# First adder convolution of an image network: TensorE's other work moved to the borders of groups, a group's near slots put side by side, its banks emptied behind the first slot

## The chip, the cores and the metric

The kernel runs on one core of one Trainium2 chip. Its time is the device time of one execution in microseconds, as the median of several runs; lower is better. Beside it there is one profiled execution, from which all durations of instructions are read.

## The reference

Four layers follow each other on an input of 4 images with 128 channels of 64x64. The diff touches the second one (an adder network block), and of that its first half:

```python
def shift_conv(x, w, stride=1):
    wq = shift_quant(w)                       # weights rounded to powers of two
    return lax.conv_general_dilated(x, wq, window_strides=(stride, stride), ...)   # 3x3, pad 1

def adder_conv(x, w):                         # out = -sum |patch - weight|, 3x3, pad 1
    patches = lax.conv_general_dilated_patches(x, filter_shape=(K, K), ...)
    p = patches.reshape(N, Ck, H * W)
    wf = w.reshape(Cout, Ck)
    def per_channel(wc):
        return -jnp.sum(jnp.abs(p - wc[None, :, None]), axis=1)
    out = lax.map(per_channel, wf)
    return out.transpose(1, 0, 2).reshape(N, Cout, H, W)

out = adder_conv(shift_conv(x, w_shift1, stride=1), w_add1)
out = jax.nn.relu(batchnorm(out, bn1_gamma, bn1_beta))
out = adder_conv(shift_conv(out, w_shift2, stride=1), w_add2)
```

So for each location and output channel the absolute differences between 128 x 9 values and weights are summed.

## The kernel before

**Splitting the sum.** A value that lies outside the range of its channel's weights contributes a term that is linear in the weights; only a "live" value, inside the range, needs relu(weight + value) worked out for all 1152 weights (9 taps x 128 output channels) of its channel. Few values are live. `sparse_adder` (L648 to L786) works on that: 32 blocks of 512 locations (8 per image), each of four groups of 128 locations, 128 groups in all. The result of a group is a table of 128 locations x 1152 (tap, output channel), in three PSUM banks of 384 columns.

**What a group does on TensorE.**

- `add_linear` (L601): nine matmuls in bf16, three parts of the weights times three banks, which open the banks.
- `add_near` (L586): for each of four near slots, the l-th live value of every channel in each of four windows of 32 locations. Four "distances" (relu(weight + value), 128x1152) are made by `distance` (L570), two on VectorE (L580) and two on ScalarE (L578), and 12 matmuls add them. These use a quarter of the array's columns each (the form 128*32 in the profile), all others use 128*128. A float32 matmul leaves two records in the profile, so a slot has 24 records.
- `add_far` (L595): three matmuls for live values beyond the four slots, with weights gathered by an indirect DMA from POOL (`weights_of`, L522) and one more distance, on VectorE for even groups and on ScalarE for odd ones.
- `closed` (L609): ScalarE empties the three banks into `ts`, with the group's totals as bias.
- `combine` (L625): nine or twelve matmuls (18 or 24 records) shift `ts` by its taps and add it to an output bank; 4 groups of an image later VectorE finishes the output block (`finished`, L725).

The pool of banks for the tables has five buffers and a group opens three, so the third bank of a group is the first of the group before it. Distances lie in two rings of six buffers, one for each engine: an engine can be three slots ahead of TensorE.

**What finds the live values.** While the four groups of a block run, `found` (L705) prepares the next block, in steps that are taken from a generator between two distances. On TensorE there are the shift convolution (`convolved`, L688, 27 matmuls in bf16), the totals (`totals`, L552), the places in the list (`listed`, L466 to L468) and the list itself (32 small matmuls, L501). On VectorE there are the copy of the convolution (L701), the ranks (L421 to L430), the list's masks and counts (L454 to L464), the totals' operand (L556), the maxima (L471, L472), the near slots (L541 to L545), then, once TensorE has given the places, chairs, fields, value, lanes and the far pattern. `thirds` (L284) splits the input of the block after that into three bf16 parts, by two casts on ScalarE (L289) and two subtractions on VectorE (L290), in turn.

**What sets the order.** Everything in this stage is recorded in program order for its engine, and each engine works through its queue in that order. `beside` (L756) is called after each of the 17 distances of a group and takes steps of `found` at a rate of 88 steps per 68 distances:

```python
                due += of * 88.0 / per
                while due >= 1.0:
                    due -= 1.0
                    next(steps, None)
```

A step that waits for TensorE stands `AFTER = 8` empty steps behind the matmuls that it waits for. TensorE's pieces of `found` go where their step falls, ahead of the near slot whose distances are being made. The closing and the combining of the group before stand behind the second near slot. `found`, the totals, the places and the list share one PSUM bank (`ps_c`).

Of the kernel before, what the change touches and what calls it, by code (L numbers as in the profile page):

```python
# [20 lines left out]
P = 128  # L21
# [262 lines left out]
def thirds(tc, pool, x, name, bufs=2):  # L284

    nc, then = tc.nc, tc.keep_in_program_order
    parts = [pool.tile(x.shape, BF16, tag=f"third{i}", bufs=bufs, name=f"{name}_{i}") for i in range(3)]
    for i in range(2):
        then(nc.scalar.copy(parts[i], x))  # L289
        then(nc.vector.tensor_tensor(x if i == 0 else parts[2], x, parts[i], ALU.subtract))  # L290
    return parts
# [16 lines left out]
TC = TAPS * P // 3  # L308


class Sparse:
# [104 lines left out]
    def ranks(self, q, v):  # L416

        nc, then, u = self.tc.nc, self.tc.keep_in_program_order, f"{self.tag}{q}"
        shape = [P, BK]
        below = self.kp.tile(shape, BF16, tag="below", name=f"below{u}")  # L420
        then(nc.vector.tensor_scalar(below, v, self.low, 2.0, ALU.is_ge, ALU.mult))  # L421
        yield
        t = self.tp.tile(shape, F32, tag="t0", name=f"live{u}")
        then(nc.vector.scalar_tensor_tensor(t, v, self.high, below, ALU.is_gt, ALU.is_gt))
        yield
        rank = self.tp.tile(shape, F32, tag="t1", name=f"rank{u}")
        then(nc.vector.tensor_tensor_scan(rank, self.inside[32], t, 0.0, ALU.mult, ALU.add))
        yield
        near = self.tp.tile(shape, F32, tag="t2", name=f"near{u}")
        then(nc.vector.tensor_tensor(near, rank, t, ALU.mult))  # L430
        yield
        yield below, near
# [12 lines left out]
    def listed(self, q, v, near, counts):  # L445
# [20 lines left out]
        pb = self.ps_c.tile([P, 2, GROUPS], F32, tag="cv", name=f"pbase{u}")  # L466
        then(nc.tensor.matmul(pb[:, 0, :], self.before, full, start=True, stop=False, skip_group_check=True))
        then(nc.tensor.matmul(pb[:, 1, :], self.cm.ones, full, start=False, stop=True, skip_group_check=True))  # L468
        at, where = new(data, "at8"), new(data, "where", U32)
        for j in range(GROUPS):  # L470
            then(nc.vector.max(at[:, j, :], masked[:, bass.ts(j, P)]))  # L471
            then(nc.vector.max_index(where[:, j, :], at[:, j, :], masked[:, bass.ts(j, P)]))  # L472
            yield
            yield
        crowded = self.crowded[:, GROUPS * q : GROUPS * (q + 1)]
        then(nc.vector.tensor_scalar(crowded, pb[:, 1, :], float(P), None, ALU.is_gt))
        base = new(small, "base")
        then(nc.vector.scalar_tensor_tensor(base, crowded, 1000.0, pb[:, 0, :], ALU.mult, ALU.add))
        then(nc.vector.tensor_tensor(counts[:, GROUPS * q : GROUPS * (q + 1)], crowded, count, ALU.mult))
        yield  # L480
        wide = [P, GROUPS, TOP + P]
        chairs = self.lp.tile(wide, BF16, tag="chairs", bufs=2, name=f"chairs{u}")
        then(nc.vector.tensor_tensor(
            chairs, self.chair.unsqueeze(1).broadcast_to(wide), base.unsqueeze(2).broadcast_to(wide), ALU.is_equal
        ))
        yield
# [11 lines left out]
        then(nc.vector.tensor_scalar(what[..., 4], valid, self.lane, None, ALU.mult))  # L498
        yield
        pl = self.ps_c.tile([P, GROUPS, FIELDS], F32, tag="cv", name=f"plist{u}")  # L500
        for j in range(GROUPS):  # L501
            for l in range(TOP):
                then(nc.tensor.matmul(
                    pl[:, j, :], chairs[:, j, TOP - l : TOP - l + P], what[:, j, l, :], start=(j + l == 0),
                    stop=(j == GROUPS - 1 and l == TOP - 1), skip_group_check=True,
                ))
            yield
        for _ in range(AFTER):
            yield
# [9 lines left out]
        yield  # L519
        yield value, lanes, hot  # L520
# [9 lines left out]
    def slots(self, q, v, key, ranks, size, tag, bufs):  # L530

        nc, then, u = self.tc.nc, self.tc.keep_in_program_order, f"{self.tag}{q}"
        n, nw = len(ranks), BK // size
        hot = self.kp.tile([P, n, BK], F32, tag=f"hot{tag}", bufs=bufs, name=f"hot{tag}{u}")
        at = self.kp.tile([P, n, nw], F32, tag=f"at{tag}", bufs=bufs, name=f"at{tag}{u}")
        step = 2
        for l0 in range(0, n, step):
            m = min(step, n - l0)
            hp = self.kp.tile([P, step, BK], F32, tag="hp", bufs=1, name=f"hp{tag}{u}_{l0}")
            for l in range(l0, l0 + m):  # L540
                then(nc.vector.tensor_scalar(hot[:, l, :], key, ranks[l], 2.0, ALU.is_equal, ALU.mult))  # L541
                yield
                then(nc.vector.scalar_tensor_tensor(hp[:, l - l0, :], key, ranks[l], v, ALU.is_equal, ALU.mult))
                yield
            then(nc.vector.tensor_reduce(  # L545
                at[:, l0 : l0 + m, :].rearrange("p l w -> p (l w)"),
                hp[:, :m, :].rearrange("p l (w j) -> p (l w) j", j=size), AX.X, ALU.add,
            ))
            yield
        yield hot, at  # L550

    def totals(self, q, v, below):  # L552

        nc, then, u = self.tc.nc, self.tc.keep_in_program_order, f"{self.tag}{q}"
        sp = self.tp.tile([P, BK], F32, tag="t0", name=f"sp{u}")
        then(nc.vector.scalar_tensor_tensor(sp, below, 1.0, v, ALU.subtract, ALU.mult))  # L556
        yield
        pt = self.ps_c.tile([P, GROUPS], F32, tag="cv", name=f"ptot{u}")
        for j in range(GROUPS):
            then(nc.tensor.matmul(  # L560
                pt[:, j : j + 1], sp[:, bass.ts(j, P)], self.cm.one_col, start=(j == 0), stop=(j == GROUPS - 1),
                skip_group_check=True,
            ))
        for _ in range(AFTER):
            yield
        total = self.kp.tile([P, GROUPS], F32, tag="total", name=f"total{u}")
        then(nc.vector.tensor_copy(total, pt))
        yield total
# [32 lines left out]
    def add_linear(self, t, lhs):  # L601

        for i, part in enumerate(self.w3):
            for y in range(3):
# [42 lines left out]

def sparse_adder(tc, cm, sp, x_d, wqs, stats, counts, p_d, y_d, tag):  # L648
# [9 lines left out]
    with ExitStack() as ctx:  # L658
# [23 lines left out]
        def split(q):  # L682
            if q < blocks:
                parts[q] = thirds(tc, xin_pool, xins.pop(q), f"{tag}x3{q}")

        split(0)

        def convolved(q):  # L688
            xins[q + 2] = fetch(q + 2)
            here = parts.pop(q)  # L690
            b, k = divmod(q, NB)
            pc = sp.ps_c.tile([P, BK], F32, tag="cv", name=f"{tag}pc{q}")
            for t in range(TAPS):
                shifted(tc, pc, wqs, here, t)
                yield
            split(q + 1)
            yield
            for _ in range(AFTER):
                yield
# [3 lines left out]
            yield v  # L703

        def found(q):  # L705

            def last_of(g):
                v = None
                for v in g:
                    if v is None:  # L710
                        yield
                got.append(v)

            got = []
            yield from last_of(convolved(q))
            v, = got
            yield from last_of(sp.ranks(q, v))
            below, near = got[1]
            yield from last_of(sp.totals(q, v, below))
            yield from last_of(sp.slots(q, v, near, near_ranks, 32, "n", 2))  # L720
            yield from last_of(sp.listed(q, v, near, counts))
            value, lanes, hot = got[4]
            ready[q] = (below, got[2], *got[3], value, lanes, hot)
# [14 lines left out]
        per = (S_NEAR * 4 + 1) * GROUPS  # L738

        ripe = []  # L740

        def combined(m, t, total):
            b, n = divmod(m, N // P)
            sp.combine(b, n, sp.closed(t, m, total))
            ripe.extend([AFTER, b, k] for k in sp.done(n))

        steps, due = iter(()), 0.0
        for m in range(groups):
            q, j = divmod(m, GROUPS)
            if j == 0:  # L750
                for _ in steps:
                    pass
                below, total, hot_n, at_n, value, lanes, hot_l = ready.pop(q)
                steps = found(q + 1) if q + 1 < blocks else iter(())

            def beside(of):  # L756
                nonlocal due
# [5 lines left out]
                due += of * 88.0 / per  # L763
                while due >= 1.0:
                    due -= 1.0
                    next(steps, None)

            t = sp.open_rows(m)
            weights = sp.weights_of(lanes[:, j : j + 1], m)
            sp.add_linear(t, below[:, bass.ts(j, P)])  # L770
            for l in range(S_NEAR):
                rs = []
                for g in range(4):
                    w = 4 * j + g
                    rs.append(sp.distance(g % 2 == 1, at_n[:, l, w : w + 1], f"n{m}_{l}_{g}"))
                    beside(1)
                sp.add_near(t, lambda g: hot_n[:, l, P * j + 32 * g : P * j + 32 * g + 32], lambda g: rs[g], False)
                if l == 1 and waiting is not None:
                    combined(*waiting)
            r = sp.distance(m % 2 == 1, value[:, j : j + 1], f"l{m}", weights)  # L780
            beside(1)
            sp.add_far(t, hot_l[:, j, :], r, False, True)
            waiting = (m, t, total[:, j : j + 1])
        combined(*waiting)
# [4 lines left out]
def sparse_rest(tc, cm, sp, left, stats, p_d, y_d, tag):  # L789
# [5 lines left out]
    with ExitStack() as ctx:  # L795
# [4 lines left out]
        with tc.For_i(0, left, F):  # L800
            with ExitStack() as inner_ctx:
# [3 lines left out]
                for q in range(B * NB):  # L805
# [3 lines left out]
                    *_, (_, near) = sp.ranks(f"r{q}", v)  # L809
# [4 lines left out]
                    *_, (hot, at) = sp.slots(f"r{q}", v, far, ranks, P, "f", 1)  # L814
# [100 lines left out]
class Sorted(Sparse):  # L915
# [75 lines left out]
    def arranged(self, s, wqs, load):  # L991
# [4 lines left out]
        def fetch(k):  # L996
# [9 lines left out]
            def third():  # L1006
                landed()
                return thirds(self.tc, self.xp, t, f"x3{u}_{k}", 1)
# [1784 lines left out]
```

## Time and profile before

| | us |
|---|---|
| median of 3 runs | 13672.89 (13670.84 to 13677.84) |
| the profiled execution | 13709.18 |
| its span, first to last instruction | 13707.2 |
| mean granted TensorE clock of that execution | 0.951 |
| near slots of the first adder convolution, first to last | 2055.3 to 4228.3 |
| in 3500 to 4000: TensorE busy | 482.39 |
| in 3500 to 4000: VectorE busy | 342.64 |
| in 3500 to 4000: ScalarE busy | 347.80 |
| in 3500 to 4000: POOL busy | 40.83 |
| in 3500 to 4000: granted clock | 1.00 |

The profile's lines name the engine (PE is TensorE, PEld its weight loads, DVE VectorE, ACT ScalarE, SP the queue that issues most DMAs), the line of the kernel, the operation, what it writes and reads, and the number of records. The ends of matmuls are modelled, so durations on PE are best read from one start to the next. In brackets stands the idle time of the engine before the line and what ended it. The profiled execution takes 36 us longer than the median of the runs, so durations summed from it are set against its own time.

### The profile page before, as it was taken

The numbers are of one execution on the slowest core, as the hardware profiler recorded it, in microseconds if no ns is written. First come the engines' busy times: TensorE is split into PE (matmuls) and PEld (weight loads), VectorE is DVE, ScalarE is ACT, GpSimd is POOL, SyncE is SP. The second block draws the span as 40 slices with busy tenths as digits, with TensorE's granted clock in tenths as the row PEclk, the third lists the DMA queues.
The fourth block names the chain that finished last, engine by engine and source line by source line (L and its number), as shares of the span: only waits on it lengthen the run. The fifth ranks groups of instructions, "written<-read, shape, count | busy, mean of one in ns | idle before, by whom it ended". The sixth has DMA issues, their size and how long they took to land. (4 is left out here: it accounts for less than half of the span.)

```text
span 13707.2 us, 216839 instructions
## 1 busy us (share of the span) xinstructions
PE 12566.8 (92%) x85293; PEld 5394.1 (39%) x85320; DVE 10865.7 (79%) x15976; ACT 8956.8 (65%) x10214; POOL 4407.8 (32%) x2328
## 2 busy tenths in 40 slices
PE   9999989999996999999999999997778869999998
PEld 3444434444443334334533444444233223333332
DVE  7788776666664888887888788885886789999997
ACT  5666646666663778776777678884333456676676
POOL 5666650000001001001000200001000159999998
PEclk9999989999997999999999999998887689999999
DMA  0000001111112101011110211114011378999997
GB/s 17 11 5 11 4 18 49 48 48 48 48 45 56 36 27 47 30 36 54 63 38 25 74 58 55 57 51 125 15 17 44 128 215 237 254 254 254 249 259 202
DMA packets 388833, 1134.65 MB, mean 83 GB/s; under 512 B 143317, under 2 KB 171792, under 8 KB 315980
## 3 DMA queue, kind: packets, MB, share of 16 engines
q1 hardware_dynamic: 322332, 857.60, 21.4%
q0 software_dynamic: 65312, 260.86, 6.2%
q8 instruction: 676, 11.08, 0.3%
q14 instruction: 369, 3.02, 0.1%
q10 hardware_dynamic: 144, 2.10, 0.0%
HBM read 910.21 MB, written 202.38 MB: 81 GB/s over the span
## 5 line engine op out<-in xcount | busy, mean ns | idle before, releaser
L1330 PE MATMUL ta<-ra,a2pick 128*32 128x384 f32 x33024 | 3098.5, 494 | 88.6 <-DVE ra L580 37.4
L578 ACT ACTIVATE ra<-a2wa,vc 128x1152 f32<-128x1152 f32 x2219 | 2686.8, 1251 | 699.1 <-PE ta L1330 635.4
L580 DVE TENSOR_SCALAR ra<-a2wa,vc 128x1152 f32<-128x1152 f32 x3285 | 2529.8, 817 | 525.1 <-PE ta L1330 456.8
L2454 PE MATMUL mg<-h,ident 128*128 128x512 f32 x4096 | 1959.4, 616 | 203.3 <-ACT m L2463 164.7
L2439 DVE TENSOR_TENSOR_SCAN h<-da,h,dbu 128x1024 f32<-128x1024 f32 x768 | 1804.3, 2349 | 118.6 <-ACT da L2425 27.4
L1330 PEld LDWEIGHTS ta<-ra,a2pick 128*32 128x32 f32 x33024 | 1155.3, 110 | 1684.1 <-issue 1307.3
L578 ACT ACTIVATE ra1n<-a1wa,atna 128x1152 f32<-128x1152 f32 x1024 | 1227.3, 1248 | 595.9 <-PE ta L590 580.6
L191 POOL TENSOR_TENSOR ssum<-ssum,et 128x512 f32<-128x512 f32 x960 | 1230.1, 1281 | 232.9 <-ACT et L186 166.2
L2454 PEld LDWEIGHTS mg<-h,ident 128*128 128x128 f32 x4096 | 726.2, 191 | 1438.3 <-ACT m L2463 688.9
L2467 POOL TENSOR_TENSOR m<-m,C 128x2048 f32<-128x2048 f32 x256 | 1157.6, 4532 | 101.5 <-ACT m L2463 74.5
L2418 POOL TENSOR_TENSOR dbu<-du,B 128x2048 f32<-128x2048 f32 x256 | 1157.8, 4538 | 90.4 <-DMA du<-du_d 39.1
L580 DVE TENSOR_SCALAR ra1n<-a1wa,atna 128x1152 f32<-128x1152 f32 x1024 | 806.8, 815 | 415.5 <-PE ta L590 396.5
L590 PE MATMUL ta<-ra1n,hotna 128*32 128x384 f32 x12288 | 1089.5, 489 | 13.0 <-DVE ra1n L580 13.0
L525 POOL DMA_INDIRECT wla<-in_w_add,lanes x156 | 187.1, 1200 | 2794.6 <-DVE lanes L1302 1738.0
L154 PE MATMUL pe<-q,k 128*128 128x512 f32 x2048 | 1051.1, 596 | 8.6 <-DVE mx L164 8.1
L197 PE MATMUL pav<-et,vT 128*128 128x512 f32 x2048 | 1042.0, 593 | 1.5 <-ACT et L186 1.5
L1330 PE MATMUL ta<-ra,hot 128*32 128x384 f32 x10368 | 993.3, 495 | 35.3 <-ACT ra L578 29.1
L156 ACT COPY et<-pe 128x512 f32<-128x512 f32 x1024 | 596.5, 583 | 591.5 <-PE pe L154 575.8
L164 DVE TENSOR_TENSOR mx<-pe,mx 128x512 f32<-128x512 f32 x992 | 680.7, 686 | 335.5 <-ACT et L156 332.2
L578 ACT ACTIVATE ra<-a2wa,at 128x1152 f32<-128x1152 f32 x696 | 839.0, 1251 | 134.1 <-PE ta L1330 124.2
L580 DVE TENSOR_SCALAR ra<-a2wa,at 128x1152 f32<-128x1152 f32 x1032 | 791.1, 815 | 84.8 <-PE ta L1330 80.8
L2425 ACT ACTIVATE da<-dl,af 128x1024 f32<-128x1024 f32 x512 | 572.5, 1118 | 414.3 <-DVE h L2439 331.8
(482 smaller groups left out, 16621.6 us busy)
## 6 DMA issues: line engine op xcount, KB each, us to landing
dl<-delta_d SPq DMA_DIRECT2D x256, 512.0 KB
dl<-delta_d SPq DMA_DIRECT2D x512, 256.0 KB
du<-du_d SPq DMA_DIRECT2D x256, 512.0 KB
du<-du_d SPq DMA_DIRECT2D x512, 256.0 KB
taps_d<-tsa SPq DMA_DIRECT2D x82, 576.0 KB
sz_d<-sz SPq DMA_DIRECT2D x64, 256.0 KB
xs_d<-xs SPq DMA_DIRECT2D x8, 2048.0 KB
delta_d<-dv SPq DMA_DIRECT2D x32, 512.0 KB
```

The lines of the kernel that those rows point to most:

```text
L154: nc.tensor.matmul(pe, k[:, bass.ts(j, P)], unit[u, "q"], start=True, stop=True)
L164: nc.vector.tensor_tensor(mx, pe, mx, ALU.max)
L191: nc.gpsimd.tensor_tensor(unit[u, "sum"], unit[u, "sum"], at, ALU.add)
L197: nc.tensor.matmul(unit[u, "av"], image[u // NB][2][:, j, :], at, start=(j == 0), stop=(j == NJ - 1))
L578: then(nc.scalar.activation(r, w, AF.Relu, bias=at))
L580: then(nc.vector.tensor_scalar(r, w, at, 0.0, ALU.add, ALU.max))
L590: self.tc.keep_in_program_order(self.tc.nc.tensor.matmul(t[y][32 * g : 32 * g + 32, :], lhs(g), rhs(g)[:, bass.ts(y, TC)], start=first, st ...
L1330: self.raw(self.tc.nc.tensor.matmul(t[y][32 * g : 32 * g + 32, :], lhs, r[:, bass.ts(y, TC)], start=first, stop=False, skip_group_check=Tr ...
L2418: then(nc.gpsimd.tensor_tensor(t, du, by_states(tiles[n][0], 0, h), ALU.mult))
L2439: then(nc.vector.tensor_tensor_scan(t[:, cols][:, s], da[:, s], st[n, "dbu", h][:, cols][:, s], 0.0 if e % 4 == 0 else st["last"], ALU.mul ...
L2454: then(nc.tensor.matmul(pm, cm.ident, st[n, way, h][:, bass.ts(k, BK)], start=(way == 0), stop=(way == 1)))
L2467: then(nc.gpsimd.tensor_tensor(m, m, by_states(tiles[n][0], 1, h), ALU.mult))
```

## The change

The change rewrites how a block's preparation is laid among the group's work. Its parts:

1. The generator's steps get tokens. A `Stream` holds the generator; a step that yields `TENSOR` is left until the border before the next group, where `go` runs it. After TensorE work (unless it ends in `FREE`) and after `HELD` no step is taken until `HOLD = 12` further distances are made. The empty `AFTER` steps within `found` are gone.
2. The convolution's 27 matmuls stand together at the border before a block's first group. Totals and places share one PSUM tile and stand at one border, the list's 32 matmuls at another. In the built program these are the borders before the first, third and fourth group of a block.
3. VectorE's steps between them are taken at 1.5 per distance (in place of 88/68), and in another order: maxima and totals' operand ahead of the near slots, the near slots and the split of the next input (now a generator, `in_thirds`, a step for each of its four instructions) before the border at which the places are computed, the fields before the totals and the chairs.
4. The closing of the group before stands behind the first near slot in place of the second. Its combining moves to the border before the next group, so one group later than its closing.
5. `add_linear` goes bank by bank, each with its three parts, in place of part by part over the banks.

The other callers (`sparse_rest`, the second adder convolution's arrangement) run the same generators straight through, with the same instructions. The diff, cut to what bears on this:

```diff
+TENSOR, HELD, FREE = "tensor", "held", "free"
+HOLD = 12
+class Stream:
+    def __init__(self, work, item=None):
+        self.work, self.item = work, item
+        self.tensor, self.at, self.until, self.over = False, 0, 0, False
+    def go(self, at):
+        was = self.tensor
+        token = next(self.work, StopIteration)
+        self.over = token is StopIteration
+        self.tensor = token is TENSOR
+        if was:
+            self.at = at
+        if (was and token is None) or token is HELD:
+            self.until = self.at + HOLD
+    def step(self, at):
+        if self.over or self.tensor or at < self.until:
+            return False
+        self.go(at)
+        return True
...
-def thirds(tc, pool, x, name, bufs=2):
+def in_thirds(tc, pool, x, name, bufs=2):
...
         then(nc.scalar.copy(parts[i], x))
+        yield
         then(nc.vector.tensor_tensor(x if i == 0 else parts[2], x, parts[i], ALU.subtract))
+        yield
...
     def listed(self, q, v, below, near, counts, between):
...
+        sp = self.tp.tile([P, BK], F32, tag="t0", name=f"sp{u}")
+        then(nc.vector.scalar_tensor_tensor(sp, below, 1.0, v, ALU.subtract, ALU.mult))
+        yield
         at, where = new(data, "at8"), new(data, "where", U32)
...
+        near_slots = yield from between
+        yield TENSOR
+        pb = self.ps_c.tile([P, 3, GROUPS], F32, tag="cv", name=f"pbase{u}")
...
+        yield FREE
...
+        yield HELD
+        total = self.kp.tile([P, GROUPS], F32, tag="total", name=f"total{u}")
+        then(nc.vector.tensor_copy(total, pb[:, 2, :]))
...
+        yield TENSOR
         pl = self.ps_c.tile([P, GROUPS, FIELDS], F32, tag="cv", name=f"plist{u}")
...
-        for i, part in enumerate(self.w3):
-            for y in range(3):
+        for y in range(3):
+            for i, part in enumerate(self.w3):
...
+            yield TENSOR
             pc = sp.ps_c.tile([P, BK], F32, tag="cv", name=f"{tag}pc{q}")
             for t in range(TAPS):
                 shifted(tc, pc, wqs, here, t)
-                yield
-            split(q + 1)
-            yield
-            for _ in range(AFTER):
-                yield
...
+            def between():
+                near_slots = yield from sp.slots(q, v, near, near_ranks, 32, "n", 2)
+                yield from split(q + 1)
+                return near_slots
+            v = yield from convolved(q)
+            below, near = yield from sp.ranks(q, v)
+            ready[q] = yield from sp.listed(q, v, below, near, counts, between())
...
-                due += of * 88.0 / per
+                due = min(due + 1.5, 2.0)
                 while due >= 1.0:
                     due -= 1.0
-                    next(steps, None)
+                    steps.step(made)
+            if closed is not None:
+                combined(*closed)
+            if steps.tensor:
+                steps.go(made)
             t = sp.open_rows(m)
...
-                if l == 1 and waiting is not None:
-                    combined(*waiting)
+                if l == 0 and waiting is not None:
+                    closed = waiting[0], sp.closed(waiting[1], waiting[0], waiting[2])
...
-        combined(*waiting)
+        combined(*closed)
+        combined(waiting[0], sp.closed(waiting[1], waiting[0], waiting[2]))
```

## The prediction

> **What bounds the kernel now.** I went from the slices of the span to the stage that the diff touches (the first adder convolution, near slots from 2055 to 4228 us), then to its waits, to TensorE in one block of four groups, and to VectorE in the same block. In the waits of 2100 to 4200 us (total, times, longest):
>
> ```profile
> ACT ra1n L578 <- PE ta L590: 567.8, 303, 5.3
> DVE ra1n L580 <- PE ta L590: 385.4, 183, 7.4
> PE ta L605 <- ACT tsa L615: 60.7, 29, 2.1
> PEld ta L590 <- DVE ra1n L580: 59.6, 129, 1.2
> PE ta L590 <- DVE ra1n L580: 13.0, 27, 0.5
> ```
>
> ScalarE and VectorE wait for TensorE to free ring buffers, TensorE rarely for them: TensorE is the bound. Its own waits are one per block at the linear matmuls (third bank not emptied yet) and short ones for VectorE. One block, TensorE's timeline (start, us, line, records):
>
> ```profile
> 3011.68 3.44 PE L298 MATMUL a1pc<-a1x,a1wq 128*128 128x512 bf16 x15
> 3015.05 2.14 PE L590 MATMUL ta<-ra1n,hotna 128*32 128x384 f32 x24
> 3017.12 2.79 PE L298 MATMUL a1pc<-a1x,a1wq 128*128 128x512 bf16 x12
> ...
> 3021.91 2.94 PE L638 MATMUL oa<-a1shift,tsa 128*128 128x64 f32 x24
> 3024.79 4.08 PE L590 MATMUL ta<-ra1n,hotna 128*32 128x384 f32 x48
> 3028.80 2.20 PE L597 MATMUL ta<-ra1l,hotla 128*128 128x384 f32 x6
> 3030.83 1.63 PE L605 MATMUL ta<-a1w,belowa 128*128 128x384 bf16 x9
> ...
> 3047.95 3.04 PE L590 MATMUL ta<-ra1n,hotna 128*32 128x384 f32 x28
> 3051.47 2.13 PE L590 MATMUL ta<-ra1n,hotna 128*32 128x384 f32 x20 [0.48 <-DVE ra1n L580]
> ...
> 3079.19 1.30 PE L605 MATMUL ta<-a1w,belowa 128*128 128x384 bf16 x7 [2.09 <-ACT tsa L615]
> 3080.32 2.18 PE L298 MATMUL a1pc<-a1x,a1wq 128*128 128x512 bf16 x5
> ```
>
> The block lasts 3080.32 - 3011.68 = 68.64 us. One near slot (24 records) takes 2.07 to the next start, two 4.01: a slot is 1.94, and leaving the near form costs 0.13. Linear takes 1.47 before other full-array work and 1.56 before a near slot: entering costs 0.09. So each near stretch costs 0.22 beyond its work; the block has ten. Two stalls are in it: the linear ones from 3076.61 to 3080.32 take 3.71 (2.24 too long), the near pair from 3047.95 to 3053.53 takes 5.58 (1.57 too long). Work without stalls: 68.64 - 3.81 = 64.83.
>
> VectorE's steps for the next block, in the same stretch:
>
> ```profile
> 3019.95 0.69 DVE L701 TENSOR_SCALAR a1p<-a1pc 128x512 f32<-128x512 f32 x1 [1.19 <-PE a1pc L298]
> 3022.74 1.22 DVE L427 TENSOR_TENSOR_SCAN ranka<-a1inside,livea 128x512 f32<-128x512 f32 x1
> 3034.49 0.68 DVE L543 SCALAR_TENSOR_TENSOR hpna<-neara,a1p 128x512 f32<-128x512 f32 x1
> 3036.88 1.22 DVE L545 TENSOR_REDUCE atna<-hpna 128x32 f32<-128x1024 f32 x1
> ```
>
> From one start to the next where nothing waits: L701 0.73, L421 0.52, L424 0.80, L427 1.25, L430 0.61, L454 0.44, L457 0.61, L460 to L464 1.20, L556 0.60, one pair of L471 and L472 0.60, L541 0.33, L543 0.60, L545 1.13, L290 0.76 (0.85 to its end); a distance 0.73 on VectorE (0.82 to its end), 1.15 on ScalarE (1.24). From L701 (3019.95) to the last L472 (3050.41) they lie over 30 us.
>
> The granted clock in windows of 3.41 us round that linear stall (busy us by engine, then the clock):
>
> ```profile
> 3077.07:3080.48 3.41, 1.32 (x9) 0.78 (x8) 2.60 (x4) 2.56 (x5) 0.00 (x0) 1.00 0.00 0
> 3080.48:3083.89 3.41, 3.41 (x10) 1.20 (x8) 0.52 (x1) 1.89 (x2) 0.00 (x0) 0.50 0.00 0
> ```
>
> A window with TensorE busy for 1.32 us is followed by one at half clock: the 15 convolution matmuls that begin it take 5.04 (3080.32 to 85.36) in place of 3.37. Six windows of the stage idle for 2.09 us, and each is followed so; of those idle 1.97 or less, none is.
>
> **The change, part by part.** *Near slots of a group in one stretch.* The built program issues per block four near stretches of 48 matmuls (96 records), against ten. Saved: 6 x 0.22 = 1.33. TensorE's work is the same otherwise: the two totals matmul groups only merge. Work per block: 64.83 - 1.33 = 63.50.
>
> *Banks emptied behind the first slot, linear by bank.* The closing on ScalarE stands behind two distances of the new group, not four, and the third bank is used six matmuls later, not two. Far takes 2.03 and its first bank is done after a third of it, so the closing runs beside far, combining and linear: the 2.24 stall goes to 0. ScalarE has room: eight or nine distances of 1.15 and three closings of 0.48 are under 12 us of the group's 16.
>
> *VectorE's steps.* This is the term that decides. They now come at 1.5 per distance (before 88/68 = 1.29) and without the 24 empty steps, 12 distances behind the convolution. In the built order of VectorE, L701 stands behind the third slot's distances of the block's first group, and from there to the last distance of its second group stand 16.8 us of steps and 11 distances (8.0 us). I walk the queues from the end of the convolution at 0; VectorE's distance waits for the slot three back plus 0.2 (a slot from 3001.92 to 3003.86 let VectorE go at 3004.08). A to D name the first to the fourth slot.
>
> First group: TensorE does linear until 1.56, A until 3.50, B until 5.43, C until 7.37. VectorE, held since before by the wait at L701, does L701 and L421 until 1.45, then D's first distance, which waits for A: 3.69 to 4.42. Then live, scan, near, away until 7.53, and D's second distance is ready at 8.35. TensorE, at 7.37, starts D at 8.3 (stall 0.9), ends it at 10.4. masked, counts, L556: far's distance starts at 10.66, is ready at 11.5 (stall 1.2). Far ends at 13.6, combining (2.8) at 16.4, linear of the second group at 17.9, A at 19.8. VectorE: the four maxima and three distances until 16.0 with one hot; B's second distance ready at 20.2 (0.3). B ends at 22.0. Two hp, one hot, a distance and L545 end at 23.45, the first L290 at 24.3; ScalarE's second cast stands behind it, and C's fourth distance behind that cast: 24.35 + 0.65 + 1.24 = 26.25, so C starts at 26.2 (stall 4.2). D's fourth waits 0.4 more for ScalarE. Sum of stalls 0.9 + 1.2 + 0.3 + 4.2 + 0.4 = 7.0; without ScalarE's cast C would start at 25.0, so 5.6 is the low end; the high end is 7.9, if the 11 distances overlapped nothing (0.09 more each). I take 6.9. Later VectorE is free again: the next wait on TensorE (totals, lists) has 12 distances between.
>
> Per block: 63.50 + 6.9 = 70.4 against 68.64: +1.8 (from +0.5 to +2.9). 31 blocks have a next one: +55 (+15 to +90). At the three image borders blocks of before last 66.4 to 66.9, since they combine less; here VectorE sets that stretch, so 2 us each are lost: +6. Before the first block nothing hides the second split: two casts of 0.74 and two L290 of 0.85, and the merged totals: +4 (0 to 5).
>
> *The clock.* A gap of 4 us cut anywhere by windows of 3.41 leaves at least 2.0 in one of them, which the rows put at the edge of halving; no row shows such a gap in this stage. Price per block from 0 (no halving) to 1.7 (as 5.04 - 3.37); the mean over all positions of the gap is 1.4, of which the 0.4 of D is absorbed, so I take 1.1: 31 x 1.1 = +34 (0 to 53). The six halvings of before go: -10. [...]
>
> *The rest at nothing:* gathers (POOL, 1.3 us each): lanes are known some 29 us before the far distance that needs the rows, and no wait of the stage is on their DMA; gone, it would be the time to landing, which no row shows. The fetch now stands before the first gather on POOL: one memset of 0.67, under the same 29 us. On SP fetch, store of p and store of y keep their order. Both last groups' combining at the end: under 1 us. No other stage changes its order.
>
> Sum: 55 + 6 + 4 + 34 - 10 = +89 on a profiled 13709.18 (span 13707.2, 2.0 around it); the runs' median is 36 lower, and I take the sum over to it: 13672.89 + 89 = **13762**.
>
> **The rivals.** *The cushion holds.* If VectorE gets through the dense stretch without holding TensorE, the block falls to 63.5 plus at most 0.4: 31 x -4.9, +4, -10, so about -158: 13515. For it: VectorE is busy 46.9 us of a block's 68.6, and its ring lets it run three slots ahead. Against: the ring is full just when it stands at L701, and 24.8 us of queue plus 2.2 of waiting meet 21.6 us of TensorE's work until D of the second group. It decides from 68.64 - 63.50 = 5.1 us of stall per block downward. *Stalls without halving:* +89 - 34 = +55: 13728; for it the gap may be shorter than walked. *A draw:* stalls of 4.5 to 5.5: 13673 within 27. *The matmuls aren't gathered:* excluded by the built order.
>
> **How the numbers follow.** Forecast (stalls and halving) 0.60, stalls alone 0.24, cushion holds 0.11, draw 0.05. A difference under 0.2% (27 us) is what can't be told from none. Faster 0.11, same 0.05, slower 0.84. Low end: +0.9 per block without halving, 28 + 10 - 10: 13701; high end: 90 + 6 + 5 + 53 - 10 = 144, which needs every term high, so I stop at 13805.
>
> **What would show it.** In the waits: linear on the closing gone; near slots waiting for both VectorE's and ScalarE's distances, 4 us at the third slot of every second group of a block, far waiting for VectorE; VectorE waiting some 9 us per block for the convolution at the step that is L701 now; half clock about 31 times; blocks of 70 to 72 us. Wrong: blocks of 64 us, or a longest near wait under 2 us.

## The result, and the profile after

The changed kernel is slower: 13762.33 us (median of 5 runs, 13748.59 to 13773.2) against 13677.84 (5 runs, 13670.84 to 13693.12), a ratio of 1.0059, interval 1.0045 to 1.0072.

```profile
span 13770.7 us, 216609 instructions
...
PE 12569.3 (91%) x85293; PEld 5410.4 (39%) x85320; DVE 10864.8 (79%) x15976; ACT 8953.1 (65%) x10214; POOL 4361.8 (32%) x2328
```

This is the head of the page of after. TensorE has the same 85293 matmul records as before, and its busy time is 2.5 us above before's 12566.8. Busy time holds what the gathering saves and what a slower clock adds (the convolution's 15 matmuls took 5.04 us at half clock in before, 3.37 at full clock), so it does not say where the loss lies; the rows below do. Where the two profiled executions differ:

| stretch | before | after | difference |
|---|---|---|---|
| start to the first near slot of this convolution | 2055.4 | 2059.7 | +4.3 |
| first near slot to the last one | 2172.5 | 2259.7 | +87.2 |
| last near slot to the end | 9479.4 | 9451.3 | -28.1 |
| span | 13707.2 | 13770.7 | +63.5 |

The third row cannot be put down to the change: in the profiled executions of the kernels below this stretch takes 9437 us (e1, which has the old arrangement), 9445 to 9451 (e2 to e4), 9487 (e6) and 9513 (e5), so it varies by more than 28 us from one execution to another. Before's one profiled execution was also long against its own median.

The lines moved: L612 is the near line that was L590, L619 far (L597), L627 linear (L605), L660 combining (L638), L300 the convolution (L298), L602 and L600 the distances on VectorE and ScalarE (L580, L578), L289 and L291 the casts and subtractions of the split, L730 VectorE's copy of the convolution (L701). The waits of after in 2100 to 4200 us (us in total, times, longest):

```profile
ACT ra1n L600 <- PE ta L612: 290.1, 88, 6.6
DVE a1p L730 <- PE a1pc L300: 246.5, 29, 8.5
DVE ra1n L602 <- PE ta L612: 228.9, 178, 3.1
...
ACT a1x L289 <- DVE a1xin L291: 179.8, 29, 7.4
PEld ta L612 <- DVE ra1n L602: 150.8, 142, 2.5
...
PE ta L612 <- DVE ra1n L602: 63.7, 64, 1.8
...
PE ta L619 <- DVE ra1l L602: 29.1, 29, 1.0
```

TensorE no longer waits for ScalarE's closing at the linear matmuls. It now waits for VectorE, at the near slots and at far, and VectorE stands 8.5 us in each block waiting for the convolution. The first two groups of a block on TensorE's timeline, with the start of the third (start, us, line, records; the weight loads that wait inside a run are not shown, so a run can be longer than its work):

```profile
3053.73 6.05 PE L300 MATMUL a1pc<-a1x,a1wq 128*128 128x512 bf16 x27
3059.62 1.63 PE L627 MATMUL ta<-a1w,belowa 128*128 128x384 bf16 x9
3061.17 6.64 PE L612 MATMUL ta<-ra1n,hotna 128*32 128x384 f32 x76
3068.05 2.13 PE L612 MATMUL ta<-ra1n,hotna 128*32 128x384 f32 x20 [0.23 <-DVE ra1n L602]
3071.18 2.20 PE L619 MATMUL ta<-ra1l,hotla 128*128 128x384 f32 x6 [1.01 <-DVE ra1l L602]
3073.22 2.84 PE L660 MATMUL oa<-a1shift,tsa 128*128 128x64 f32 x24
3075.90 1.63 PE L627 MATMUL ta<-a1w,belowa 128*128 128x384 bf16 x9
3077.45 5.66 PE L612 MATMUL ta<-ra1n,hotna 128*32 128x384 f32 x52
3084.89 0.83 PE L612 MATMUL ta<-ra1n,hotna 128*32 128x384 f32 x2 [1.77 <-DVE ra1n L602]
3086.09 5.64 PE L612 MATMUL ta<-ra1n,hotna 128*32 128x384 f32 x42 [0.37 <-ACT ra1n L600]
3091.65 2.20 PE L619 MATMUL ta<-ra1l,hotla 128*128 128x384 f32 x6
...
3099.18 7.95 PE L612 MATMUL ta<-ra1n,hotna 128*32 128x384 f32 x96
3107.06 2.20 PE L619 MATMUL ta<-ra1l,hotla 128*128 128x384 f32 x6
...
3125.39 6.05 PE L300 MATMUL a1pc<-a1x,a1wq 128*128 128x512 bf16 x27
```

The third group shows a near stretch without a stall: 96 records, 7.88 us to the start of far. The first group's takes 3071.18 - 3061.17 = 10.01, so 2.13 is lost; the second group's takes 3091.65 - 3077.45 = 14.20, so 6.32 is lost. The block takes 3125.39 - 3053.73 = 71.66. From block to block it lies between 71.63 and 71.72, 71.67 in the mean.

What stands before the gap of the second group, on VectorE and ScalarE:

```profile
3082.14 1.21 DVE L585 TENSOR_REDUCE atna<-hpna 128x32 f32<-128x1024 f32 x1
3083.27 0.83 DVE L291 TENSOR_TENSOR a1xin<-a1xin,a1x 128x660 f32<-128x660 f32 x1
3084.02 0.81 DVE L602 TENSOR_SCALAR ra1n<-a1wa,atna 128x1152 f32<-128x1152 f32 x1
3084.13 0.74 ACT L289 CAST a1x<-a1xin 128x660 bf16<-128x660 f32 x1 [6.05 <-DVE a1xin L291]
3084.78 3.55 ACT L600 ACTIVATE ra1n<-a1wa,atna 128x1152 f32<-128x1152 f32 x3
```

VectorE's distance for the third slot ends at 3084.83, and the two records of L612 start at 3084.89. ScalarE's distance of the same slot stands behind a cast that itself waited 6.05 us for VectorE's subtraction; that distance starts at 3084.78 and takes about 1.2, and the next records start at 3086.09.

The clock in windows of 3.41 us round this gap (stretch; length, busy us of PE, PEld, DVE, ACT, POOL, each with its records; then the granted clock, the DMA share and GB/s):

```profile
3079.05:3082.46 3.41, 3.27 (x34) 1.07 (x28) 3.41 (x7) 0.00 (x0) 0.00 (x0) 1.00 0.00 0
3082.46:3085.87 3.41, 1.49 (x6) 0.14 (x2) 3.33 (x5) 1.74 (x2) 0.00 (x0) 1.00 0.00 0
3085.87:3089.29 3.42, 3.20 (x21) 0.99 (x25) 3.25 (x11) 3.42 (x4) 0.00 (x0) 0.50 0.42 96
```

The window after the gap runs at half clock. The stage has 30 such windows, before's had 6. Of the 30, one lies in the first block and 29 stand behind this gap, one in each of the next 29 blocks.

### The profile page after: what moved, and what is told of

The parts are those of the page before. It is cut to its first block, busy times and chain, and to the rows that moved or that the text cites. A ratio compares the mean times of both kernels' runs of the same rounds, so it can differ in the third digit from the quotient of the medians.

```text
span 13770.7 us, 216609 instructions
## 1 busy us (share of the span) xinstructions
PE 12569.3 (91%) x85293; PEld 5410.4 (39%) x85320; DVE 10864.8 (79%) x15976; ACT 8953.1 (65%) x10214; POOL 4361.8 (32%) x2328
## 5 line engine op out<-in xcount | busy, mean ns | idle before, releaser
L600 ACT ACTIVATE ra<-a2wa,vc 128x1152 f32<-128x1152 f32 x2219 | 2688.0, 1251 | 657.5 <-PE ta L1356 638.1
L1356 PE MATMUL ta<-ra,a2pick 128*32 128x384 f32 x33024 | 3048.3, 492 | 60.5 <-DVE ra L602 36.7
L602 DVE TENSOR_SCALAR ra<-a2wa,vc 128x1152 f32<-128x1152 f32 x3285 | 2526.1, 816 | 483.9 <-PE ta L1356 477.7
L600 ACT ACTIVATE ra1n<-a1wa,atna 128x1152 f32<-128x1152 f32 x1024 | 1210.2, 1245 | 318.0 <-PE ta L612 318.0
L612 PE MATMUL ta<-ra1n,hotna 128*32 128x384 f32 x12288 | 1165.9, 504 | 82.2 <-DVE ra1n L602 68.4
L602 DVE TENSOR_SCALAR ra1n<-a1wa,atna 128x1152 f32<-128x1152 f32 x1024 | 802.4, 816 | 282.0 <-PE ta L612 259.6
L600 ACT ACTIVATE ra<-a2wa,at 128x1152 f32<-128x1152 f32 x696 | 838.2, 1251 | 134.3 <-PE ta L1356 123.7
L602 DVE TENSOR_SCALAR ra<-a2wa,at 128x1152 f32<-128x1152 f32 x1032 | 790.9, 815 | 84.9 <-PE ta L1356 82.7
```

Of the source, the lines that this page charges most:

```text
L600: then(nc.scalar.activation(r, w, AF.Relu, bias=at))
L602: then(nc.vector.tensor_scalar(r, w, at, 0.0, ALU.add, ALU.max))
L612: self.tc.keep_in_program_order(self.tc.nc.tensor.matmul(t[y][32 * g : 32 * g + 32, :], lhs(g), rhs(g)[:, bass.ts(y, TC)], start=first, st ...
L1356: self.raw(self.tc.nc.tensor.matmul(t[y][32 * g : 32 * g + 32, :], lhs, r[:, bass.ts(y, TC)], start=first, stop=False, skip_group_check=Tr ...
```

## The experiments

The theory to test: VectorE's bunched steps make the gaps (the split of the next input the largest), the gap makes the half clock, and the parts on banks cost nothing. Its rivals: the gap without the clock explains it; the split is not what decides; the banks' parts are what costs. The first four kernels ran on one chip with a shared before of 13675.2 us (13663.97 to 13682.0), the last two on another with 13727.4 (13718.15 to 13739.77), so they are compared by ratio. Blocks are given without the first one and those at the borders of images; the windows are those between the stage's first and last near slot in the profiled execution.

| kernel | median us (runs) | ratio to before, interval | us per block | half-clock windows |
|---|---|---|---|---|
| e1_banks_alone | 13587.79 (4) | 0.9935, 0.9919 to 0.9952 | 66.33 | 0 |
| e2_split_later | 13665.85 (10) | 0.9993, 0.9984 to 1.0003 | 68.12 to 68.22 | 2 |
| e3_gap_filled | 13739.93 (4) | 1.0044, 1.0027 to 1.0061 | 70.43 to 70.54 | 1 |
| e4_banks_undone | 13762.38 (4) | 1.0064, 1.0047 to 1.0080 | 70.44 to 71.59, the last 15 71.67 | 24 |
| e5_spread | 13592.27 (4) | 0.9897, 0.9881 to 0.9914 | 64.08 | 0 |
| e6_ring8 | 13724.14 (10) | 0.9998, 0.9988 to 1.0008 | 68.05 to 69.40 | 16 |

**e1: the kernel before, with the banks' parts alone.** Nothing is gathered; the closing goes one slot forward and linear goes by bank.

```diff
-        for i, part in enumerate(self.w3):
-            for y in range(3):
+        for y in range(3):
+            for i, part in enumerate(self.w3):
...
+                if l == 0 and waiting is not None:
+                    closed = waiting[0], sp.closed(waiting[1], waiting[0], waiting[2])
                 if l == 1 and waiting is not None:
-                    combined(*waiting)
+                    combined(*closed)
...
```

> The kernel before with two parts of the change alone: the closing behind the first near slot (the combining stays behind the second), and the linear matmuls bank by bank. Theory (the linear stall of 2.24 us per block is ScalarE's order, and nothing takes its place): blocks of 66.4 us in place of 68.64, the wait of linear on the closing gone, no half-clock windows in the stage; 31 x -2.24 and six halvings of 1.7 less: -79, so 13598, ratio 0.994. Rival (ScalarE is late by its load, so the wait only moves to the next near slot): blocks of 68 to 69 us, ratio 0.998 to 1.002.

Measured 0.9935 and blocks of 66.33, 2.32 less than before's 68.65. On TensorE's timeline linear now takes 1.47 to the start of the next run, where before's linear took 3.71 at this place:

```profile
3040.26 1.63 PE L605 MATMUL ta<-a1w,belowa 128*128 128x384 bf16 x9
3041.73 3.44 PE L298 MATMUL a1pc<-a1x,a1wq 128*128 128x512 bf16 x15
```

So in the old order the banks' parts are a gain of their own: the 2.24 of the linear stall, and with it the halvings.

**e2: the split of the next input behind the places' border.** All else as changed.

```diff
         yield FREE
+        yield from after
...
                 near_slots = yield from sp.slots(q, v, near, near_ranks, 32, "n", 2)
-                yield from split(q + 1)
...
-            ready[q] = yield from sp.listed(q, v, below, near, counts, between())
+            ready[q] = yield from sp.listed(q, v, below, near, counts, between(), split(q + 1))
```

> The changed kernel with the split of the next input (two casts on ScalarE, two subtractions on VectorE) behind the places' border, so out of VectorE's dense stretch; all else as changed. Theory (the third slot of every second group waits for ScalarE's distance behind the second cast, behind VectorE's queue): that wait falls from 4.2 to 2.2 us, the fourth slot's 0.4 goes, and a gap of 2.2 rarely idles a clock window enough to halve the next; blocks of 68.2 in place of 71.67, 31 x -3.5 = -107: 13655. Rival 1 (the same, but half-clock windows stay): blocks of 69.4: 13690. Rival 2 (the stretch isn't bound by VectorE's queue): no change, 13762.

Measured blocks of 68.12 to 68.22 and two halvings, and a ratio that cannot be told from 1. TensorE's timeline (near is L613 here, far L620, VectorE's distance L603):

```profile
3025.68 2.20 PE L620 MATMUL ta<-ra1l,hotla 128*128 128x384 f32 x6 [1.01 <-DVE ra1l L603]
...
3031.95 5.66 PE L613 MATMUL ta<-ra1n,hotna 128*32 128x384 f32 x52
3038.62 4.06 PE L613 MATMUL ta<-ra1n,hotna 128*32 128x384 f32 x44 [1.01 <-DVE ra1n L603]
3042.61 2.20 PE L620 MATMUL ta<-ra1l,hotla 128*128 128x384 f32 x6
```

The second group's near stretch takes 3042.61 - 3031.95 = 10.66: 2.78 is lost in place of 6.32. ScalarE's distance is no longer late there, VectorE's still is: it starts at 3037.76, right behind the last reduction of the near slots (3036.63). The first group, which the split doesn't touch, still waits 1.01 at far. With the halving that it brings about, the split was over half of the second group's loss (3.54 of 6.32); what is left of the gap is followed by a half-clock window in one block alone.

**e3: the gap kept, but TensorE busy in it.** Sixteen matmuls with a zero stationary operand, which add nothing to the sums, stand before the third slot of the second group of each block.

```diff
+        zero = zero_pool.tile([P, P], BF16, name=f"{tag}zero")
+        nc.vector.memset(zero, 0.0)
...
+                if j == 1 and l == 2:
+                    for i in range(16):
+                        then(nc.tensor.matmul(t[i % 3], zero, sp.w3[0][:, 0:TC], start=False, stop=False, skip_group_check=True))
```

> The changed kernel with 16 more matmuls (a stationary operand of zeros, which adds nothing to the table) ahead of the third near slot of every second group of a block, where TensorE waits 4.2 us; they take 16 x 0.16 = 2.6 us of that wait and two changes of form 0.22. Theory (halving costs, and comes from the gap): no half-clock windows, blocks of 70.4 in place of 71.67, 31 x -1.2 = -37: 13725. Rival 1 (the half clock only falls where VectorE binds anyway): half-clock windows go but the time stays, 13762 within 10. Rival 2 (the gap has other causes and the added work comes on top): blocks of 73 to 74, 13810 to 13850.

TensorE's timeline:

```profile
3059.72 4.68 PE L612 MATMUL ta<-ra1n,hotna 128*32 128x384 f32 x48
3064.34 2.78 PE L807 MATMUL ta<-a1w,a1zero 128*128 128x384 bf16 x16
3067.04 0.95 PE L612 MATMUL ta<-ra1n,hotna 128*32 128x384 f32 x6
3068.36 2.14 PE L612 MATMUL ta<-ra1n,hotna 128*32 128x384 f32 x24 [0.37 <-ACT ra1n L600]
...
3072.71 2.20 PE L619 MATMUL ta<-ra1l,hotla 128*128 128x384 f32 x6
```

ScalarE's distance lets TensorE go on 3068.36 - 3059.72 = 8.64 after the group's first slot, to the hundredth as in after (3086.09 - 3077.45): the fill neither shortens nor lengthens the gap. But the near stretch takes 12.99, not 14.20, the block about 70.45 instead of 71.67, and of the 30 windows at half clock only the one in the first block is left. So an ordinary block loses 1.21 by the clock, and 5.11 of the second group's 6.32 is the wait itself. A block of e4 that happens not to be halved shows the same 12.99 with nothing in the gap:

```profile
3070.12 5.66 PE L612 MATMUL ta<-ra1n,hotna 128*32 128x384 f32 x52
...
3083.11 2.20 PE L619 MATMUL ta<-ra1l,hotla 128*128 128x384 f32 x6
```

Block by block, the 29 blocks that are halved in after take 33.1 us less in e3, 1.14 each in the mean: 1.16 to 1.24 in most, 0.56 or 0.57 in the three at image borders. The time fell less than expected, to 13740 and not 13725. Two things on record explain it. From the last convolution on there is no such gap, and the fill comes on top: 122.4 us to the last near slot, in after 118.9. So the near stage is 29.6 us shorter than after's, not 33. And the number of halvings is not fixed: after's profiled execution is the slowest of its five, while e4, which ran on e3's chip and has after's median, has 24 half-clock windows in its profiled execution and a near stage 22.2 us longer than e3's. The medians of e4 and e3 differ by 22.

**e4: the changed kernel without the banks' parts.** The closing goes back behind the second slot, linear part by part.

```diff
-        for y in range(3):
-            for i, part in enumerate(self.w3):
+        for i, part in enumerate(self.w3):
+            for y in range(3):
...
-                if l == 0 and waiting is not None:
+                if l == 1 and waiting is not None:
                     closed = waiting[0], sp.closed(waiting[1], waiting[0], waiting[2])
```

> The changed kernel with the banks' two parts undone: closing behind the second near slot again, linear part by part over the banks. Theory (with combining and the other work at the border and the casts no longer ahead of the closing, linear comes late enough in either order): no wait of linear on the closing, blocks of 71.7, 13762 within 15. Rival (this order is what removed the stall, as the prediction put it): linear waits up to 2.24 us per block again, 13800 to 13830.

The time is that of the changed kernel. In the waits of 2100 to 4200 us TensorE does not wait at linear (L627) here either; its longest are these:

```profile
PE ta L612 <- DVE ra1n L602: 63.7, 64, 1.8
...
PE ta L619 <- DVE ra1l L602: 29.2, 29, 1.0
```

In the gathered order the banks' parts change nothing that could be measured. Combining stands between far and linear there, 2.7 us that the closing gains (3073.22 to 3075.90 in after); that this is what covers it is argued from the order, not tried by itself.

**e5: the steps spread.** The split and the four pairs of maxima go behind the places' border, the rate falls from 1.5 steps per distance to 1.0, and `HOLD` from 12 distances to 9.

```diff
-HOLD = 12
+HOLD = 9
...
         at, where = new(data, "at8"), new(data, "where", U32)
-        for j in range(GROUPS):
-            then(nc.vector.max(at[:, j, :], masked[:, bass.ts(j, P)]))
-            then(nc.vector.max_index(where[:, j, :], at[:, j, :], masked[:, bass.ts(j, P)]))
-            yield
...
         yield FREE
+        for j in range(GROUPS):
+            then(nc.vector.max(at[:, j, :], masked[:, bass.ts(j, P)]))
+            then(nc.vector.max_index(where[:, j, :], at[:, j, :], masked[:, bass.ts(j, P)]))
+            yield
+        yield from after
...
-                yield from split(q + 1)
...
-                due = min(due + 1.5, 2.0)
+                due = min(due + 1.0, 2.0)
```

> The changed kernel with VectorE's steps spread: the split and the four pairs of maxima (neither is needed for the places) behind the places' border, one step per distance in place of 1.5, and a hold of 9 distances in place of 12. Theory (what the gathered order lost it lost in VectorE's dense stretch): 12.7 us of steps in place of 16.8 lie between the convolution's copy and the places, the waits of near slots and far on VectorE sum to about 0.7 us per block in place of 6.9, no half-clock windows; blocks of 64.2 us in place of 68.64 before, 31 x -4.4 +6 +4 -10 = -136: 13540, ratio 0.990. Rival (spreading only moves VectorE's late point into the third or fourth group, or into the list's border): blocks of 66 to 68, ratio 0.995 or above, with waits of the third and fourth group's slots in the profile.

Blocks of 64.08, no halving, ratio 0.9897: the fastest of all, and its interval lies wholly below e1's. The ratio is as forecast; the median is 52 us above 13540, on a chip where before is 55 us above the prediction's. The first two groups of a block on TensorE's timeline:

```profile
3021.03 7.95 PE L613 MATMUL ta<-ra1n,hotna 128*32 128x384 f32 x96
3029.36 2.20 PE L620 MATMUL ta<-ra1l,hotla 128*128 128x384 f32 x6 [0.38 <-DVE ra1l L603]
...
3035.63 8.37 PE L613 MATMUL ta<-ra1n,hotna 128*32 128x384 f32 x96
3043.93 2.20 PE L620 MATMUL ta<-ra1l,hotla 128*128 128x384 f32 x6
```

These are the same two groups that lost 2.13 and 6.32 in after; here they lose 0.45 (8.33 to far) and 0.42 (8.30). VectorE still stands at its copy of the convolution, up to 9.2 us per block. That wait costs next to nothing here, with what follows it spread. Which of the three edits does how much was not separated.

**e6: rings of eight distances in place of six.**

```diff
-        sp.pools(ctx, 6)
+        sp.pools(ctx, 8)
```

> The changed kernel with eight buffers in each ring of distances in place of six, so that VectorE can stand four slots ahead when it comes to the convolution's copy. Theory (the ring sets the cushion): the block's first group no longer waits (0.9 at its fourth slot and 1.2 at far go), the third slot of the second group still waits 4.2 for the second cast, so the half-clock windows stay; blocks of 69.3 to 69.5 in place of 71.67, 31 x -2.3 = -70: 13690. Rival (the cushion doesn't matter, VectorE's rate over the whole block does): no change, 13762.

TensorE's timeline:

```profile
3021.63 7.95 PE L612 MATMUL ta<-ra1n,hotna 128*32 128x384 f32 x96
3029.51 2.20 PE L619 MATMUL ta<-ra1l,hotla 128*128 128x384 f32 x6
...
3042.94 6.38 PE L612 MATMUL ta<-ra1n,hotna 128*32 128x384 f32 x44 [1.77 <-DVE ra1n L602]
```

One slot more of lead clears the first group altogether (7.88 to far). In the second one the third slot still waits. The block shown is a halved one, 3049.25 - 3035.78 = 13.47 to far; one without halving takes 12.72 (3104.59 to 3117.31), so the halving costs 0.75 there. The ratio comes back to 0.9998, which cannot be told from before. The halvings came in half the blocks only, where all were expected.

## Why the prediction was right

The direction, the time (13762 against 13762.33) and the mechanism came out as forecast. The agreement to the microsecond is luck: the medians differ by 84.5, where the sum said 89, and the before measured with the result is 5 us higher. In the profiled executions the stage itself grows by 87.2, where the sum had 85 (55, 6, 34 and -10). The terms, for an ordinary block:

| term | predicted | measured | from |
|---|---|---|---|
| TensorE's work without stalls | 63.50 | 63.22 | 71.67 - 2.13 - 6.32; 63.2 in e5 too (64.08 - 0.45 - 0.42) |
| first group's stalls | 2.1 | 2.13 | after; gone in e6 |
| second group's stalls | 4.9 | 5.11 | e3; 2.78 without the split (e2) |
| half clock | 1.1 | 1.21 | e3 against after; 1.14 in the mean of the 29 halved blocks |
| sum | 71.5 (stalls taken as 6.9) | 71.67 | |

*The near slots in one stretch* save what was said and a little more; 18 records of combining take 2.01 here and took 2.11 before, when they stood behind a near run.

*The linear stall* went to zero, but the step named the wrong cause. The prediction credited it to the closing behind the first slot and to linear by bank. Those parts can do it: e1 shows that they are worth 0.65% where nothing else does it. But e4 has neither and no such stall, so the gathered order removes it without them. The term was right in size because the change removes the stall twice over.

*VectorE's queue* was the deciding step, and the walk through it held to 0.3 us or better at the points that the rows show: the first group's fourth slot goes on 8.43 after the convolution's end (8.3 forecast, counted from 3059.62), far 11.56 after it (11.5), the second group's first slot 17.83 (17.9), its third slot 26.47 (26.2), released first by VectorE and 1.2 us later by ScalarE's distance behind the second cast. VectorE waits 8.5 us at the copy of the convolution, 9 forecast.

*The clock.* Of the 31 blocks in the sum, 29 were halved at this gap, for 33.1 us together where 34 were forecast. The size is right, but the edge from which it was derived does not carry over. In before, windows with TensorE idle for 2.09 us are followed by half clock and those with 1.97 or less are not, as here with 1.45 busy of 3.41 (columns as above):

```profile
2732.33:2735.74 3.41, 1.45 (x9) 0.87 (x9) 2.60 (x4) 2.72 (x5) 0.00 (x0) 1.00 0.02 5
2735.74:2739.15 3.41, 3.41 (x21) 1.34 (x22) 0.36 (x1) 1.73 (x2) 0.00 (x0) 1.00 0.00 0
```

In after the window before the halving is idle for only 1.92 us by its records (1.49 busy of 3.41 in the one shown), and as little as 1.87 in others. The ends of matmuls are modelled, and the two lone records at 3084.89 count as 0.83 us of work where two in a run take 0.16; that may be the difference, but it is not shown, and what the clock goes by stays open. But e3, which fills the gap with 2.78 us of matmuls and changes nothing else, has 1 half-clock window in place of 30: the other 29 hang on the idle time in the gap and not on its neighbours.

*The rivals.* "Stalls without halving" falls with the 30 windows. "The cushion holds" falls with the waits, and e6 shows why: the ring of six is one slot short in the first group, and in the second one VectorE and the casts are late with eight as well. "A draw" falls with the interval of the ratio, which begins at 1.0045. *Prologue:* +4.3, forecast +4; but the first near slot comes at 2055.4 and 2056.5 in the two profiled executions with the old order (before, e1) and at 2057.0 to 2061.1 in the six with the new one, so its size is not known to better than a few us.

## What to carry to other kernels

When side work is gathered to save switches on the bounding engine, ask what its followers on the other engines now do: steps that were spread become a bunch behind one wait, and the ring's depth in slots times the slot's time (here three slots of 1.94 us) is, by an estimate from these runs, about what they may take before the bound engine stops: with a fourth slot, in e6, the first group's 2.13 us of stall is gone. Here the gathered order ends at -1% (e5) or +0.6% (after), and the difference is where VectorE's steps stand and at which rate they are taken. Most of that -1% was to be had without gathering: the banks' parts alone give -0.65% (e1). A step that passes from one engine to another and back (cast, subtraction, cast) belongs where neither queue is needed soon: moving the split there in e2 took the second group's loss from 6.32 us to 2.78.

## What was not expected of the hardware

The blocks of after fall in step with the clock's windows. A half-clock window in this trace lasts 3.413 us, and the starts of the 30 lie whole multiples of that apart. The 29 behind the gap come 71.68 apart, which is 21 times that, and the blocks keep to it within 0.05. Blocks that take 70.45, 70.53 or 71.11 in e3 all take 71.63 to 71.72 here, so each halving here costs just what its block lacks to 21 windows, and 1.21 is no fixed price. In e4 one can see it begin. Two blocks that follow each other (columns as in the windows above):

```profile
3046.40:3116.90 70.50, 66.83 (x602) 34.66 (x600) 47.06 (x92) 46.74 (x49) 4.15 (x5) 1.00 0.15 47
3116.90:3188.50 71.60, 68.09 (x601) 34.84 (x599) 47.06 (x92) 46.63 (x49) 4.15 (x5) 0.98 0.15 46
```

The first has no halving and takes the 70.45 of the filled gap. The second has one, and from there on all 15 blocks take 71.65 to 71.72, so that the gap stays at its place in the window and each block is halved again. It need not hold: earlier in the same trace three halvings (at 2224.01, 2295.69 and 2367.37) and later two (2794.03, 2865.71) also came 71.68 apart, but their blocks took 71.26 to 71.59, and the next blocks were not halved. That the phase is held because 21 windows fit is argued from these lengths, not tried. In e6 a block without halving takes 68.05 to 68.14, a little under 20 windows (68.27). There halvings come up to three in a row, 68.27 apart, then stop for some blocks, 16 in all. So in these traces the price of a halving (0.56 to 1.24 us in after, 0.75 in e6) and the number of windows at half clock (30 in after, 24 in e4, 16 in e6) differ with how the block's length lies to the windows. That the one sets the other is the author's reading; no run changes the length alone.
